# Odd exponentials of a graph attention kernel in two half tiles, added by two GpSimd instructions

## The chip, the cores and the metric

The kernel runs on one core of a Trainium2 chip. The metric is the device time of one execution in microseconds (us), the median of several runs. The engines are named as in the profile: PE is TensorE, DVE VectorE, ACT ScalarE, POOL GpSimd and SP SyncE, which issues DMAs.

## The reference

16 graphs of 1024 nodes with 256 features each, and a 0/1 adjacency matrix for each. Two layers follow each other, layer 0 with 4 heads of 64 features and layer 1 with 8 heads of 32. Each is a masked attention on the normalized input, added to the input:

```python
def gnn(h, adj, Wq, Wk, Wv, Wo, bo):          # per head; D = 64 or 32
    q, k, v = h @ Wq, h @ Wk, h @ Wv          # layer 1: each with a bias
    s = where(adj == 1, q @ k.T / sqrt(D), -inf)
    return concat(softmax(s) @ v) @ Wo + bo

h = relu(layernorm(x));  x = x + gnn(h, adj, *layer0)
h = relu(layernorm(x));  x = x + gnn(h, adj, *layer1)
```

All is in float32.

## The kernel before

**Steps.** For each graph and layer the queries are cut into two halves of 512 and the heads into two groups (class `Group`). Scores are kept transposed, keys on the partitions and queries along the row, so that their exponentials are at once the operand of the product with the values. A step (class `Step`) has four blocks of 128 keys x 512 queries. In layer 0 a group has two heads and a step takes two key tiles; in layer 1 a group has four heads and a step takes one key tile. A group has 4 steps in layer 0 and 8 in layer 1; `st.j` counts them. Of the 768 steps 256 are of layer 0 and 512 of layer 1.

**What a step does.** `scores` (L400) writes the four blocks into two PSUM pairs of two banks each; the pool `ps_s` has three such pairs, which the projections (`pq`, `pv`, `py`) and transposes (`ph`) share. `exponentials` takes one pair after the other: L416 on DVE takes the minimum of the scores and the mask times 1e20 and writes half of the step's tile `p` in SBUF, and L421 on ACT takes the exponential in place. Two steps later (`LEAD = 2`) `weigh` (L433) multiplies the four blocks with the values into one PSUM bank `po`.

**Row sums.** The softmax's denominators are sums of the exponentials over the keys. In layer 1, `count_steps` adds the tile of each odd step onto that of the even step before it with one GpSimd instruction (L534, 128 x 2048 float32). DMAs that add (`accumulate`, L520) then gather the four sums of a group into one tile, and `count` (L301) multiplies it with a matrix of ones. In layer 0, `add_tiles` (L442 to L448) folds two steps into half a tile with DVE and GpSimd instructions.

**Buffers.** An even step's tile comes from seven buffers with the tag `p0`, as it lives until the row sums are done. An odd step's tile comes from two buffers with the tag `p1`, and is free when `weigh` and the add have read it. Before the first steps the same buffers hold the first adjacency matrix (`stage`, `stage_t`).

**Order.** Every engine's instructions stand in the order in which the program issues them; nothing reorders them. `Stream.run` issues the steps of all graphs in one stream, layer 0 of graph b + 1 in front of layer 1 of graph b, and at each step what `later` has put down for it: normalization (L173 to L190), projections, the load of adjacency rows (L128, issued by GpSimd), their transposition by DMA (L134, issued by SP), the conversion to a mask (L143 on ACT, L151 on DVE), the bias (L198, a DMA that GpSimd issues) and the division by the row sums (L341 to L352). GpSimd so has in one queue its adds, the issue of its DMAs and some small instructions, and where the first of them waits, the rest waits too.

Of the kernel before, what the change touches and what calls it, by code (L numbers as in the profile page):

```python
# [10 lines left out]
F32 = mybir.dt.float32  # L11
BF16 = mybir.dt.bfloat16
# [6 lines left out]
P = 128  # L19
# [3 lines left out]
LEAD = 2  # L23
# [59 lines left out]
def fast_program(ctx, tc, a, w, loads, chk):  # L83
# [3 lines left out]
    nc = tc.nc  # L87
    x, adj, out = a["x"], a["adj"], a["out"]
    B, N, E = x.shape
    NT = N // P  # L90
# [6 lines left out]
    pp = ctx.enter_context(tc.tile_pool(name="pp", bufs=2))  # L97
# [21 lines left out]
    class Mask:  # L119
# [10 lines left out]
        def flip(self, t, to=None):  # L130
            if to is None:
                to = adjp.tile([P, NT, P], BF16, tag="adjT", name=f"adjT_{self.b}_{t}")
            self.flipped[t] = to
            nc.sync.dma_start_transpose(to, self.src.pop(t))  # L134
# [137 lines left out]
    class Group:  # L272
# [20 lines left out]
                st.gr, st.j, st.n, st.last = self, j, f"{self.n}_{j}", j == n_j - 1  # L293
                yield st

        def count(self, p, start, stop):

            if start:
                self.s = ps_o.tile([P, 512], F32, tag="pz", name=f"pz_{self.n}")
            for r in range(self.per):  # L300
                nc.tensor.matmul(  # L301
                    self.s[r * self.D : (r + 1) * self.D, :], w.ones[:, : self.D], p[:, r, :],
                    start=start, stop=stop,
                )

        def count_added(self):
            self.count(self.t, True, True)

        def copy_out(self):
            if self.g == 0:  # L310
# [96 lines left out]
    def exponentials(st, between):  # L407


        gr = st.gr  # L410
        odd = st.j % 2
        st.p = pp.tile([P, 4, 512], F32, tag=f"p{odd}", bufs=2 if odd else 7, name=f"p_{st.n}")
        for i in range(2):
            half = st.p[:, ts(i, 2), :]
            kt = st.blocks[2 * i][1]
            nc.vector.scalar_tensor_tensor(  # L416
                out=half,
                in0=gr.mask.m[gr.qh][:, kt, :].unsqueeze(1).to_broadcast([P, 2, 512]),
                scalar=BIG, in1=st.ps[i], op0=ALU.mult, op1=ALU.min,
            )  # L420
            nc.scalar.activation(half, half, AF.Exp, scale=gr.scale)  # L421
            if i == 0:
                for f in between:
                    f()

    def weigh(st):
        gr = st.gr
        D = gr.D
        if st.j == 0:
            gr.o = ps_o.tile([P, 512], F32, tag="po", name=f"po_{gr.n}")  # L430
        for i, (r, kt) in enumerate(st.blocks):
            h = gr.g * gr.per + r
            nc.tensor.matmul(  # L433
                gr.o[r * D : (r + 1) * D, :], gr.inp.v[:, kt, h * D : (h + 1) * D],
                st.p[:, i, :], start=(kt == 0), stop=(kt == NT - 1),
            )

    def add_tiles(one, two):


        a, b = one.p[:, 0:2, :], one.p[:, 2:4, :]
        nc.vector.tensor_add(a, a, b)  # L442

        engine = nc.vector if one.j else nc.gpsimd
        engine.tensor_add(b, two.p[:, 0:2, :], two.p[:, 2:4, :])  # L445
        nc.gpsimd.tensor_add(a, a, b)  # L446
        if one.j:
            nc.gpsimd.tensor_add(a, a, one.gr.t)  # L448
        one.gr.t = a
# [9 lines left out]
    class Stream:  # L459
# [19 lines left out]
        def run(self):  # L479
# [3 lines left out]
            for i in range(n + LEAD):  # L483
# [6 lines left out]
                if i % 2 or not self.large(i):  # L490
                    for st in waiting:
                        weigh(st)
                    for st in waiting:
                        if st.gr.layer:
                            self.count_steps(i, st)
                        if st.last:
                            copies.append(st.gr.copy_out)
                            self.end_group(i, st.gr)
                    waiting = []
# [5 lines left out]
                if now:  # L505
                    exponentials(now, copies)
                else:
                    for f in copies:
                        f()
                if i % 2 and 3 <= i <= n and steps[i - 2].gr.layer == 0:  # L510
                    add_tiles(steps[i - 3], steps[i - 2])
# [10 lines left out]
        def count_steps(self, i, st):  # L522


            gr, j = st.gr, st.j
            if gr.hurry and j >= NT - 2:
                if st.last:
                    self.counted(i, gr)
                gr.count(st.p, False, st.last)
            elif j % 2:  # L530
                one = self.steps[i - LEAD - 1].p
                if not (gr.brief or gr.pairs) and j == 7:
                    self.accumulate(gr.two, gr.one)
                nc.gpsimd.tensor_add(one, one, st.p)  # L534
                if gr.pairs:
                    self.later(i + 2, gr.count, one, j == 1, st.last)
                elif j == 1:
                    gr.one = one
                elif j == 3:
                    self.accumulate(one, gr.one)  # L540
                    gr.one = one
                    if gr.brief:
                        self.later(i + 8, gr.count, one, True, False)
                elif gr.brief:
                    self.later(i + (6 if j == 5 else 4), gr.count, one, False, st.last)
                elif j == 5:
                    gr.two = one
                else:
                    self.later(i + (2 if gr.last else 3), self.accumulate, one, gr.two)
                    self.later(i + (4 if gr.last else 8), gr.count, one, True, True)  # L550

        def counted(self, i, gr):

# [34 lines left out]
    masks = [Mask(b) for b in range(B)]  # L588
# [3 lines left out]


    stage = [pp.tile([P, 4, N], BF16, tag="p0", bufs=7, name=f"adj_0{i}") for i in range(2)]
    stage_t = pp.tile([P, 4, NT, P], BF16, tag="p1", bufs=2, name="adjT_0")

    def load(u):
        masks[0].load(u, stage[u // 4][:, u % 4, :])
# [11 lines left out]

    def flip(u):
        to = stage[0][:, u % 4, :].rearrange("p (t q) -> p t q", q=P)
        masks[0].flip(u, stage_t[:, u, :, :] if u < 4 else to)

    flip(0)
    flip(1)
    open_w(1)
    inp.k(0)
# [6 lines left out]
    mask.put(1)  # L625
    inp.values(0)
    flip(2)
    open_x(1, 0)
    flip(3)
# [52 lines left out]
    for t in range(NT):  # L682
        i = 5 + 2 * t
# [207 lines left out]
def kernel(  # L891
# [28 lines left out]
    with ExitStack() as fast, tc.manual_schedule():  # L920
        fast_program(fast, tc, a, w, loads, chk)
# [61 lines left out]
```

## Time and profile before

| | us |
|---|---|
| median of 3 runs | 3335.38 |
| the runs | 3333.37 to 3335.87 |
| span of the profiled execution | 3332.6 |
| PE busy in it | 3245.0 (97%) |
| DVE busy | 2557.2 (77%) |
| POOL busy | 2387.3 (72%) |
| ACT busy | 2178.2 (65%) |
| L534, 255 instructions | 1201.7 |
| L416, 1536 instructions | 1790.7 |

The span goes from the first to the last instruction of one execution. What lies around it isn't given apart for that execution; the median of the runs is 2.8 us above the span. A row of the page's groups has the line, the engine, the operation, what is written from what, the shape and the count; then busy us and the mean ns of one; then the idle time of the engine just before them, and what ended it. The granted TensorE clock of the profiled execution was 0.993 of full speed on average.

### The profile page before, as it was taken

The page shows a single profiled execution, that of the slowest core. Times are in us where ns is not written, and L with a number is a line of the kernel's source. Part 1 is how long each engine was busy: PE and PEld are TensorE (multiplying, and loading weights), DVE is VectorE, ACT ScalarE, POOL GpSimd, SP SyncE. Part 2 cuts the span into 40 slices and gives each one's busy share as a digit, 9 for nine tenths or more (in the row PEclk, how much of TensorE's full clock was granted, in tenths as well). Part 3 has the DMA queues.
Part 4 walks back from the last instruction along what each step waited for, and adds up shares of the span by engine and source line. Part 5 has one row for each costly group of instructions (what it writes and reads, how often), then busy time and mean ns, then how long its engine had stood idle before and what let it go on. Part 6 is the DMA issues. An engine that isn't in the chain of part 4 may idle for free.

```text
span 3332.6 us, 44087 instructions
## 1 busy us (share of the span) xinstructions
PE 3245.0 (97%) x16766; PEld 1272.4 (38%) x16766; DVE 2557.2 (77%) x2760; ACT 2178.2 (65%) x2402; POOL 2387.3 (72%) x1272
## 2 busy tenths in 40 slices
PE   8999999999999999999999999999999999999898
PEld 3443343433433333333434333343343343333333
DVE  5777877878778787786878768787787877878867
ACT  5567576675766757567575666757667576675565
POOL 4568586786867868677686776868778586785766
PEclk9999999999999999999999999999999999999999
DMA  7338467383664846548375573855738467482431
GB/s 145 63 67 148 97 111 140 73 153 86 121 128 82 157 83 131 113 93 149 77 141 102 105 138 77 146 103 112 138 74 152 96 112 139 80 149 52 89 77 31
DMA packets 313484, 361.08 MB, mean 108 GB/s; under 512 B 190000, under 2 KB 257840, under 8 KB 290480
## 3 DMA queue, kind: packets, MB, share of 16 engines
q0 software_dynamic: 77856, 253.78, 42.1%
q1 hardware_dynamic: 235408, 104.41, 14.0%
q8 instruction: 133, 2.18, 0.3%
q14 instruction: 87, 0.71, 0.1%
HBM read 119.54 MB, written 17.56 MB: 41 GB/s over the span
## 4 chain that ended last, share of the span: by engine, by line
PE 73%; POOL 8%; DMA 7%; DVE 5%; issue 3%; ACT 3%; SPq 1%; POOLq 0%; DVEq 0%; ACTq 0%
PE ps L400 24%; PE po L433 21%; PE pq L225 11%; PE pv L262 7%; PE py L381 5%; POOL p L534 5%; DMA p<-p 4%; DVE p L416 4%; PE pz L301 3%; DMA adjT<-adj 2%; ACT p L421 1%; PE ph L208 1%; POOL p L445 1%; ACT mask L143 1%; DVE p L442 1%
## 5 line engine op out<-in xcount | busy, mean ns | idle before, releaser
L416 DVE SCALAR_TENSOR_TENSOR p<-mask,ps 128x1024 f32<-128x1024 fp8e4 x1536 | 1790.7, 1213 | 598.6 <-PE ps L400 509.9
L421 ACT ACTIVATE p<-p 128x1024 f32<-128x1024 f32 x1536 | 1616.8, 1057 | 960.6 <-DVE p L416 915.2
L534 POOL TENSOR_TENSOR p<-p,p 128x2048 f32<-128x2048 f32 x255 | 1201.7, 4714 | 181.5 <-PE po L433 162.2
L400 PE MATMUL ps<-qT,kT 32*128 32x512 f32 (+1 forms) x6144 | 1196.0, 635 | 37.4 <-DVE p L416 35.6
L433 PE MATMUL po<-p,v 128*32 128x512 f32 (+1 forms) x6144 | 994.0, 603 | 1.0 <-ACT cat L312 0.9
L400 PEld LDWEIGHTS ps<-qT,kT 32*128 32x128 f32 (+1 forms) x6144 | 382.4, 185 | 739.5 <-issue 358.6
L446 POOL TENSOR_TENSOR p<-p 128x1024 f32<-128x1024 f32 x128 | 319.7, 2497 | 273.4 <-DVE p L445 268.4
L433 PEld LDWEIGHTS po<-p,v 128*32 128x32 f32 (+1 forms) x6144 | 229.1, 118 | 691.7 <-issue 503.6
L445 POOL TENSOR_TENSOR p<-p 128x1024 f32<-128x1024 f32 x64 | 151.4, 2366 | 236.2 <-DVE p L442 151.8
L262 PE MATMUL pv<-wv,hT 128*128 128x256 f32 x1024 | 239.5, 387 | 14.6 <-ACT hT L209 14.5
L520 POOL DMA_DIRECT2D p<-p x178 | 178.8, 1005 | 98.1 <-DMA p<-p 66.1
L225 PE MATMUL pq<-hT,wk 128*128 128x512 f32 x512 | 239.6, 611 | 2.8 <-ACT hT L209 2.8
L225 PE MATMUL pq<-hT,wq 128*128 128x512 f32 x512 | 240.0, 612 | 0.1
L381 PE MATMUL py<-wo,cat 128*128 128x256 f32 x1008 | 235.8, 387 | 3.3 <-ACT hT L209 1.0
L262 PEld LDWEIGHTS pv<-wv,hT 128*128 128x128 f32 x1024 | 190.6, 191 | 88.1 <-ACT hT L209 26.8
L381 PEld LDWEIGHTS py<-wo,cat 128*128 128x128 f32 x1008 | 188.3, 191 | 74.7 <-issue 46.3
L352 POOL TENSOR_TENSOR cat<-cat,inv 128x512 f32<-128x512 f32 x127 | 178.8, 1408 | 7.5 <-DMA inv<-vd 6.3
L151 DVE TENSOR_SCALAR mask<-mask 128x1024 fp8e4<-128x1024 fp8e4 x128 | 178.6, 1395 | 0.0
L442 DVE TENSOR_TENSOR p<-p 128x1024 f32<-128x1024 f32 x128 | 161.4, 1261 | 0.0
L448 POOL TENSOR_TENSOR p<-p,p 128x1024 f32<-128x1024 f32 x64 | 152.4, 2381 | 5.0
L301 PE MATMUL pz<-p,ones 128*32 128x512 f32 (+1 forms) x888 | 148.7, 595 | 4.6 <-DMA p<-p 3.8
L225 PEld LDWEIGHTS pq<-hT,wk 128*128 128x128 f32 x512 | 93.2, 192 | 145.1 <-issue 103.5
(50 smaller groups left out, 1696.0 us busy)
## 6 DMA issues: line engine op xcount, KB each, us to landing
p<-p POOLq DMA_DIRECT2D x178, 1024.0 KB, 8.8
adj<-in_adj_dram POOLq DMA_DIRECT2D x128, 256.0 KB, 4.4
x<-bo POOLq DMA_DIRECT2D x64, 512.0 KB, 6.0
x<-in_x_dram SPq DMA_DIRECT2D x32, 512.0 KB, 4.1
inv<-vd SPq DMA_DIRECT2D x128, 128.0 KB, 2.9
inv<-vd SPq DMA_DIRECT2D x252, 64.0 KB, 2.9
out_dram<-x SPq DMA_DIRECT2D x31, 512.0 KB, 3.1
sums<-s SPq DMA_DIRECT2D x384, 2.0 KB, 3.4
```

Source lines behind the costliest of these rows:

```text
L225: nc.tensor.matmul(pq[:, m, :], wt[self.layer][:, c, ts(m, P)], self.hT[half][:, c, :], start=(c == 0), stop=(c == 1),)
L262: nc.tensor.matmul(pv[:, i, :], self.hT[half][:, c, ts(i, P)], w.v[self.layer][:, c, :], start=(c == 0), stop=(c == 1),)
L301: nc.tensor.matmul(self.s[r * self.D : (r + 1) * self.D, :], w.ones[:, : self.D], p[:, r, :], start=start, stop=stop,)
L381: nc.tensor.matmul(py[:, i, :], self.half.cat[:, c, ts(i, P)], w.o[self.layer][:, c, :], start=(c == 0), stop=(c == 1),)
L400: nc.tensor.matmul(st.ps[i // 2][:, i % 2, :], gr.inp.kT[r * D : (r + 1) * D, gr.g, ts(kt, P)], gr.inp.qT[gr.qh][r * D : (r + 1) * D, gr.g ...
L416: nc.vector.scalar_tensor_tensor(out=half, in0=gr.mask.m[gr.qh][:, kt, :].unsqueeze(1).to_broadcast([P, 2, 512]), scalar=BIG, in1=st.ps[i] ...
L421: nc.scalar.activation(half, half, AF.Exp, scale=gr.scale)
L433: nc.tensor.matmul(gr.o[r * D : (r + 1) * D, :], gr.inp.v[:, kt, h * D : (h + 1) * D], st.p[:, i, :], start=(kt == 0), stop=(kt == NT - 1),)
L442: nc.vector.tensor_add(a, a, b)
L445: engine.tensor_add(b, two.p[:, 0:2, :], two.p[:, 2:4, :])
L446: nc.gpsimd.tensor_add(a, a, b)
L534: nc.gpsimd.tensor_add(one, one, st.p)
```

## The change

In an odd step the exponentials are written into two tiles of 128 x 2 x 512 instead of one of 128 x 4 x 512, with the tags `p10` and `p11` and two buffers each, so that the memory is the same. `count_steps` adds each of them onto its half of the even step's tile with an instruction of its own. An even step keeps its one tile, and `st.halves` names its two halves. `weigh`, `count`, `add_tiles` and the first adjacency's `stage_t` read the halves in place of the whole. In the built program every other instruction keeps its place on its engine; each half add waits for TensorE and ScalarE as the whole one did, and the first and the second half of L416 in an odd step each wait for GpSimd's add of the buffer that they write.

```diff
-        def count(self, p, start, stop):
+        def count(self, halves, start, stop):
...
-                    self.s[r * self.D : (r + 1) * self.D, :], w.ones[:, : self.D], p[:, r, :],
+                    self.s[r * self.D : (r + 1) * self.D, :], w.ones[:, : self.D],
+                    halves[r // 2][:, r % 2, :],
...
-            self.count(self.t, True, True)
+            self.count([self.t], True, True)
...
-        st.p = pp.tile([P, 4, 512], F32, tag=f"p{odd}", bufs=2 if odd else 7, name=f"p_{st.n}")
-        for i in range(2):
-            half = st.p[:, ts(i, 2), :]
+        if odd:
+            st.halves = [
+                pp.tile([P, 2, 512], F32, tag=f"p1{i}", bufs=2, name=f"p_{st.n}_{i}")
+                for i in range(2)
+            ]
+        else:
+            st.p = pp.tile([P, 4, 512], F32, tag="p0", bufs=7, name=f"p_{st.n}")
+            st.halves = [st.p[:, ts(i, 2), :] for i in range(2)]
+        for i, half in enumerate(st.halves):
...
-                st.p[:, i, :], start=(kt == 0), stop=(kt == NT - 1),
+                st.halves[i // 2][:, i % 2, :], start=(kt == 0), stop=(kt == NT - 1),
...
-        engine.tensor_add(b, two.p[:, 0:2, :], two.p[:, 2:4, :])
+        engine.tensor_add(b, *two.halves)
...
-                gr.count(st.p, False, st.last)
+                gr.count(st.halves, False, st.last)
             elif j % 2:
-                one = self.steps[i - LEAD - 1].p
+                even = self.steps[i - LEAD - 1]
+                one = even.p
                 if not (gr.brief or gr.pairs) and j == 7:
                     self.accumulate(gr.two, gr.one)
-                nc.gpsimd.tensor_add(one, one, st.p)
+                for k, half in enumerate(st.halves):
+                    nc.gpsimd.tensor_add(one[:, ts(k, 2), :], one[:, ts(k, 2), :], half)
...
-    stage_t = pp.tile([P, 4, NT, P], BF16, tag="p1", bufs=2, name="adjT_0")
+    stage_t = [
+        pp.tile([P, 2, NT, P], BF16, tag=f"p1{i}", bufs=2, name=f"adjT_0{i}") for i in range(2)
+    ]
...
-        masks[0].flip(u, stage_t[:, u, :, :] if u < 4 else to)
+        masks[0].flip(u, stage_t[u // 2][:, u % 2, :, :] if u < 4 else to)
```

The other calls of `count` pass `even.halves` where they passed `one`.

More of the change, by code (lines that the diff above doesn't have):

```diff
@@ L528, in count_steps @@
                     self.counted(i, gr)
-                gr.count(st.p, False, st.last)
+                gr.count(st.halves, False, st.last)
             elif j % 2:
-                one = self.steps[i - LEAD - 1].p
+                even = self.steps[i - LEAD - 1]
+                one = even.p
                 if not (gr.brief or gr.pairs) and j == 7:
                     self.accumulate(gr.two, gr.one)
-                nc.gpsimd.tensor_add(one, one, st.p)
+                for k, half in enumerate(st.halves):
+                    nc.gpsimd.tensor_add(one[:, ts(k, 2), :], one[:, ts(k, 2), :], half)
                 if gr.pairs:
-                    self.later(i + 2, gr.count, one, j == 1, st.last)
+                    self.later(i + 2, gr.count, even.halves, j == 1, st.last)
                 elif j == 1:
@@ L542, in count_steps @@
                     if gr.brief:
-                        self.later(i + 8, gr.count, one, True, False)
+                        self.later(i + 8, gr.count, even.halves, True, False)
                 elif gr.brief:
-                    self.later(i + (6 if j == 5 else 4), gr.count, one, False, st.last)
+                    self.later(i + (6 if j == 5 else 4), gr.count, even.halves, False, st.last)
                 elif j == 5:
@@ L549, in count_steps @@
                     self.later(i + (2 if gr.last else 3), self.accumulate, one, gr.two)
-                    self.later(i + (4 if gr.last else 8), gr.count, one, True, True)
+                    self.later(i + (4 if gr.last else 8), gr.count, even.halves, True, True)
         def counted(self, i, gr):
```

## The prediction

> **What bounds the kernel now.** I read the page first: the totals, then the groups of layer 1, then the list of waits, then one stretch in order of time.
>
> ```profile
> span 3332.6 us, 44087 instructions
> ...
> PE 3245.0 (97%) x16766; PEld 1272.4 (38%) x16766; DVE 2557.2 (77%) x2760; ACT 2178.2 (65%) x2402; POOL 2387.3 (72%) x1272
> ...
> L416 DVE SCALAR_TENSOR_TENSOR p<-mask,ps 128x1024 f32<-128x1024 fp8e4 x1536 | 1790.7, 1213 | 598.6 <-PE ps L400 509.9
> ...
> L534 POOL TENSOR_TENSOR p<-p,p 128x2048 f32<-128x2048 f32 x255 | 1201.7, 4714 | 181.5 <-PE po L433 162.2
> ...
> L448 POOL TENSOR_TENSOR p<-p,p 128x1024 f32<-128x1024 f32 x64 | 152.4, 2381 | 5.0
> ```
>
> TensorE sets the end: 97% busy, nobody else over 77%. A gain has to be TensorE time. The page's last three rows give the parts: the masking on VectorE (L416), the whole-tile add that the change splits (L534), and an add of half that size (L448). The waits of VectorE show where L534 reaches the others:
>
> ```profile
> DVE p L416 <- PE ps L400: 509.9, 343, 5.0
> ...
> DVE p L416 <- POOL p L534: 83.1, 61, 3.2
> ```
>
> The columns are total us, times, longest. In 61 of the 255 cases VectorE stands before an odd step because the odd buffer, of which there are two, has not been read by GpSimd yet. What that costs TensorE is in the timeline of one such stretch (start, length, engine, line, idle time before):
>
> ```profile
> 2144.83 4.57 POOL L534 TENSOR_TENSOR p<-p,p 128x2048 f32<-128x2048 f32 x1
> ...
> 2149.43 4.61 DVE L416 SCALAR_TENSOR_TENSOR p<-mask,ps 128x1024 f32<-128x1024 fp8e4 x4 [1.54 <-POOL p L534]
> ...
> 2153.41 0.66 POOL L128 DMA_DIRECT2D adj<-in_adj_dram  x1 [4.01 <-DMA adjT<-adj]
> ...
> 2154.65 4.91 POOL L534 TENSOR_TENSOR p<-p,p 128x2048 f32<-128x2048 f32 x1
> ...
> 2155.47 1.14 PE L400 MATMUL ps<-qT,kT 32*128 32x512 f32 x8
> ...
> 2158.40 1.13 PE L400 MATMUL ps<-qT,kT 32*128 32x512 f32 x4
> ...
> 2159.15 1.63 POOL L352 TENSOR_TENSOR cat<-cat,inv 128x512 f32<-128x512 f32 x1
> 2159.59 4.61 DVE L416 SCALAR_TENSOR_TENSOR p<-mask,ps 128x1024 f32<-128x1024 fp8e4 x4 [2.79 <-POOL p L534]
> ...
> 2160.37 4.90 POOL L534 TENSOR_TENSOR p<-p,p 128x2048 f32<-128x2048 f32 x1
> ...
> 2160.87 1.13 PE L400 MATMUL ps<-qT,kT 32*128 32x512 f32 x4 [1.34 <-DVE p L416]
> ```
>
> The scores of a step are eight matmuls into two PSUM pairs. At 2155.47 both pairs were free and the eight ran side by side; the next work began 1.07 us later. At 2158.40 only one was: its four ran, then TensorE stood until VectorE had emptied the other, the second four began at 2160.87 and the next work at 2161.92. That is 3.52 us for 1.07, a loss of 2.45, though the idle column says 1.34. Added over the 512 score stretches of layer 1, the time above 1.07 is 147 us, and 72 us of it lie in the 60 stretches where VectorE's lateness goes back to a wait for L534. They come in 15 groups, one in each batch but the last, 3.4 to 6.8 us each. So 72 us is the ceiling.
>
> **What the Trainium skill says.** "Perfetto Trace Analysis", Identifying Performance Opportunities: an equal gap that comes back again and again can mean too few buffers. The trace agrees: two odd buffers, 61 waits. The same page, Optimizing Scalar/DVE Operations, says that if an engine isn't saturated but causes bubbles on others, cutting its instructions up may let work finish sooner; that is the change's pattern, said there of other engines. "GPSIMD Engine Reference", Performance versus the Vector engine, has 4497 ns for an add of 2048 float32 columns; here the shortest L534 took 4525 ns. "Advanced Engine Details and Errata", VectorE Performance Modes, says GpSimd and VectorE's two-port instructions block each other. The trace has that at L151: 661 ns at the shortest, 8427 at the longest, the latter ending 0.6 us after an L534 had.
>
> **The change, part by part.**
>
> *The adds.* 255 adds of 2048 columns become 510 of 1024. Shortest whole add 4525 ns; shortest 1024-column add on GpSimd 2342 (L446, L445 2341, L448 2344). Two halves are 4.68, so **0.16 us more per pair**. Back to back nothing of that hides: the L534 at 2160.37 follows L352, which ended at 2160.78, and ended 4.49 after it. 255 x 0.16 = 41 us more GpSimd work, 72% to 73% busy. Outside the 15 groups it costs nothing: GpSimd then waits for TensorE (162.2 us over 111 times at L534). If that cover failed everywhere it would be the 41 us.
>
> *The release.* Call E the end of the whole add. Before, VectorE's first half starts at E and its second at E + 1.13 (four L416 in 4.61). After, the first half may start at E + 0.16 - 2.34, the second at E + 0.16. Where VectorE's wait is under 2.2 us, the first half waits no more. But the second half can't pass E, and all that follows it on VectorE's queue (the next even step, which frees the PSUM pairs of the next scores and projections) is behind it. So relative to GpSimd, VectorE wins **at most 1.13 us, and once**: the next odd step meets the next E, and E moves only if GpSimd starts earlier.
>
> *Does E move?* In the group shown it doesn't. The add at 2154.65 is queued behind L128, which waited 4.01 us for a transposing DMA that was issued at 2148.85, before the first wait of the group ended. The add at 2160.37 follows it through L352 without a break. In the group at 1939 to 1961 the add at 1950.68 is behind an accumulating DMA (L520), issued 0.6 us after the one issued at 1939.71 landed (1949.5), itself behind an add. Both are GpSimd's own chain.
>
> *Worked through for 2144 to 2168.* First wait, 1.54: E = 2149.40, first half free from 2147.2, VectorE ready at 2147.9: gone, TensorE 1.04 ahead. Second: E = 2159.56 becomes 2159.72; VectorE is ready at 2155.8, its first half starts at 2157.4, its second at 2159.72, and the following masks end 1.13 - 0.16 = 0.97 sooner than before. Third: two splits in the chain, E = 2165.27 becomes 2165.59; the values' matmuls, which take the PSUM pair of the second half, start at 2165.59 + 1.25 = 2166.84 instead of 2167.71, some 0.8 sooner. Then GpSimd catches up. Gain of the group: 1.13 - 2 x 0.16 = **0.81 us**, of 5.2 lost. Times 15: 12.2 us. I take 0.81 for all. With three splits in the chain a group gives 0.65 (10 us), with one 0.97 (14.5 us).
>
> *The rest.* The second half of L416 gets a wait of its own for GpSimd: a semaphore event of 21 ns (median), at most 384 odd steps x 21 ns = 8 us on an engine with 23% idle, taken as nothing; on the chain in the groups it is 15 x 2 x 0.02 = 0.6 us. The half-tile reads at L433 and L301 and the three-operand forms at L445 are the same instructions. SBUF is the same size, as is the order on every queue. DMAs keep number and size; L520 is issued up to 0.16 later. In the last batch two L151 stand 8.4 and 6.3 us behind GpSimd's queue; each has one split add in its way: 0.3 us more if VectorE doesn't get in between the halves, 2 x 2.3 us less if it does. I take 0.
>
> Sum: span 3332.6 - 12.2 + 0.6 = 3321.0. The median of the runs shown is 2.8 above this profile's span (3335.38), so 3323.8; I say 3323.
>
> **The rivals.**
> *Every wait shrinks by itself.* If E follows TensorE in most groups (GpSimd's gaps ahead of L128 and L520 move along), each of the 61 waits gives up the smaller of itself and 1.13 us: 51 of the 83 us of waiting. At the rate of the ceiling (72 lost for 83 waited) that is 44 us: 3291. For it: in each group GpSimd does have gaps of 2 to 4 us. Against: their releasers are DMAs.
> *Nothing to measure.* The second half is what TensorE needs next, or the pair costs 0.4 rather than 0.16, so a group gives 0 to 0.4: 3330 to 3336.
> *Slower, by the shared port.* L151 loses against GpSimd's queue when two adds follow without a gap; now there are twice as many starts, and all have shifted. One more L151 held for two instructions costs 6 to 8 us, as at 3115 and 3156. The gain of 12 is gone with two such, and it is a measurable loss from three on, out of the six L151 of the last batch that take 0.7 to 1.8 us now: 3323 + 3 x 7 = 3344. For it: those two are the longest stalls of TensorE in the trace (7.2 and 5.3 us). Against: in the other batches L151 meets the adds of layer 0, which keep their size.
> *The change doesn't do what it says*: only if the second half had to wait for the first's add; the built program has the two tiles waiting each for its own. Left at nothing.
>
> **How the numbers follow.** A measurement of this kernel tells about 0.2%, 6.7 us, from no change. One allowance a group (gain 7 to 25): 0.58. Every wait (25 to 60): 0.14. Nothing: 0.21. Shared port: 0.07. So faster 0.72, same 0.21, slower 0.07. The range 3296 to 3334 leaves out the upper end of the second case, the losses, and the last part of the third.
>
> **What would show it.** Right: L534's successor has 510 instructions near 2.36 us, some 41 us more GpSimd time; the wait of L416 for it falls well below 83 us but stays, now before second halves; the sum over score stretches drops by about 12. Wrong: that wait nearly gone and TensorE's stretches at 1.07 (second case); pairs over 4.9 us (third); a longer L151 (fourth).

## The result and the profile after

The kernel after took 3348.3 us (median of 20 runs, 3343.4 to 3360.3), the kernel before in the same comparison 3340.6 us (20 runs, 3333.4 to 3356.3). The ratio is **1.0022, with a 95% interval of 1.0010 to 1.0034**: slower by about 7.7 us. The forecast was 3323 us, with a range of 3296 to 3334. It stood on 3335.4 us for the kernel before, the median of the three runs shown above, so it was a gain of 12 us.

The profile's page of the kernel after (totals, then groups: line, engine, operation, what is written from what, shape, count | busy us, mean ns | idle us before them and what ended most of it):

```profile
span 3349.0 us, 44964 instructions
...
PE 3236.8 (97%) x16766; PEld 1272.0 (38%) x16766; DVE 2582.6 (77%) x2760; ACT 2180.3 (65%) x2402; POOL 2425.2 (72%) x1527
...
L423 DVE SCALAR_TENSOR_TENSOR p<-mask,ps 128x1024 f32<-128x1024 fp8e4 x1536 | 1794.6, 1213 | 593.7 <-PE ps L401 519.0
...
L543 POOL TENSOR_TENSOR p<-p,p 128x1024 f32<-128x1024 f32 x510 | 1245.4, 2562 | 145.9 <-PE po L440 145.9
...
L262 PE MATMUL pv<-wv,hT 128*128 128x256 f32 x1024 | 239.1, 387 | 30.2 <-DVE p L423 15.5
...
L225 PE MATMUL pq<-hT,wq 128*128 128x512 f32 x512 | 239.9, 612 | 9.6 <-DVE p L423 9.5
...
L151 DVE TENSOR_SCALAR mask<-mask 128x1024 fp8e4<-128x1024 fp8e4 x128 | 202.6, 1583 | 0.0
...
L301 PE MATMUL pz<-p,ones 128*32 128x512 f32 (+1 forms) x888 | 150.0, 602 | 21.5 <-DMA p<-p 20.6
```

The line numbers that moved: L352 is now L353, L400 is L401, L416 is L423, L442 to L446 are L449 to L453, L520 is L527 and L534 is L543. TensorE has the same matmuls and is busy 8 us less, yet the span is 16 us longer. GpSimd has 38 us more work. The last two rows are the ones to look at, since the change touches neither. Before they were:

```profile
L151 DVE TENSOR_SCALAR mask<-mask 128x1024 fp8e4<-128x1024 fp8e4 x128 | 178.6, 1395 | 0.0
...
L301 PE MATMUL pz<-p,ones 128*32 128x512 f32 (+1 forms) x888 | 148.7, 595 | 4.6 <-DMA p<-p 3.8
```

L151, a conversion of the mask on VectorE, takes 24 us more, and L301, the product with ones that gives the row sums, stands 17 us longer for the accumulating DMA.

The waits of the kernel after (total us, times, longest):

```profile
DVE p L423 <- POOL p L543: 69.8, 63, 3.3
...
PE pz L301 <- DMA p<-p: 20.6, 14, 3.7
...
PE pv L262 <- DVE p L423: 15.5, 13, 1.2
...
PE pq L225 <- DVE p L423: 9.5, 13, 1.2
```

Instruction by instruction on VectorE, the 83 us before first halves have become 25 us before first halves and 45 us before second ones. The second halves' wait comes out at `pv` and `pq`, the projections that take the PSUM pair of the second half: 1.2 us each at most. And L301 waits in 14 batches, 0.26 to 3.65 us each; before, the same 14 waits were 0.22 to 0.64 us.

Since the 16,766 matmuls stand in the same order in both traces, the intervals from one start to the next can be subtracted one by one, and the differences summed by what the later matmul writes. Before to after that gives scores -25.1 us, `pv` +15.3, `pq` +9.5, `pz` (L301) +17.4, the rest -0.9: together +16.2, nearly all of the 16.4 us between the two spans. **What the scores won, the projections gave back, and the row sums lost 17 us on top.**

### How a late GpSimd reaches the row sums

One of the 14, in order of time (start, length, engine, line, idle time before). Before:

```profile
548.41 4.53 POOL L534 TENSOR_TENSOR p<-p,p 128x2048 f32<-128x2048 f32 x1 [0.61 <-PE po L433]
...
552.90 0.59 POOL L128 DMA_DIRECT2D adj<-in_adj_dram  x1
...
553.32 2.04 DVE L151 TENSOR_SCALAR mask<-mask 128x1024 fp8e4<-128x1024 fp8e4 x1
553.50 1.30 POOL L352 TENSOR_TENSOR cat<-cat,inv 128x512 f32<-128x512 f32 x1
...
559.11 1.22 DVE L442 TENSOR_TENSOR p<-p 128x1024 f32<-128x1024 f32 x1
...
565.23 0.87 POOL L520 DMA_DIRECT2D p<-p  x1
...
572.29 1.06 PE L301 MATMUL pz<-p,ones 128*32 128x512 f32 x8 [0.23 <-DMA p<-p]
```

After:

```profile
552.13 4.96 POOL L543 TENSOR_TENSOR p<-p,p 128x1024 f32<-128x1024 f32 x2
...
555.65 3.81 DVE L151 TENSOR_SCALAR mask<-mask 128x1024 fp8e4<-128x1024 fp8e4 x1
556.76 0.85 POOL L128 DMA_DIRECT2D adj<-in_adj_dram  x1
557.36 1.54 POOL L353 TENSOR_TENSOR cat<-cat,inv 128x512 f32<-128x512 f32 x1
...
562.97 1.21 DVE L449 TENSOR_TENSOR p<-p 128x1024 f32<-128x1024 f32 x1
...
569.54 0.85 POOL L527 DMA_DIRECT2D p<-p  x1
...
577.29 1.93 PE L301 MATMUL pz<-p,ones 128*32 128x512 f32 x8 [2.89 <-DMA p<-p]
```

VectorE comes to L151 with the scores, 2.33 us later than before, as TensorE does at this point. GpSimd comes out of this multiplication (L352, L353) 4.1 us later (558.90 against 554.80), so it is 1.8 us late against TensorE: it is still in the last add of layer 1 when L151 comes. In both traces L151 ends 0.56 us after it, however long before it began. So GpSimd's 1.8 us go into L151 (2.04 to 3.81 us). Of these, 1.5 us reach the fold of layer 0 on VectorE (L442, later L449) and GpSimd's fold behind it. There GpSimd's second instruction takes 0.4 us more, and the DMA that adds takes 7.7 us from its issue to its landing in place of 7.0. TensorE, which before had waited 0.23 us at this place, now waits 2.89.

The same is found in 13 of the 14 batches (in the last one nothing changes). Their second L151 takes 0.4 to 2.2 us more, the fold behind it comes later by that less 0.1 to 0.3 us, and in nine of them L301 comes later by what the fold is late, within 0.03 us. In the other four GpSimd's fold or the DMA adds 0.5 to 1.5 us. TensorE's own time from L151 to the matmul ahead of L301 is the same in both traces. The 0.23 us is the point: the chain **already ended at TensorE in each of the 14 batches before the change**, and of what is added to it nearly all is lost.

### The profile page after: what moved, and what is told of

Its sections match the earlier page's. It is cut to its first block, busy times and chain, and to the rows that moved or that the text cites. A ratio compares the mean times of both kernels' runs of the same rounds, so it can differ in the third digit from the quotient of the medians.

```text
span 3349.0 us, 44964 instructions
## 1 busy us (share of the span) xinstructions
PE 3236.8 (97%) x16766; PEld 1272.0 (38%) x16766; DVE 2582.6 (77%) x2760; ACT 2180.3 (65%) x2402; POOL 2425.2 (72%) x1527
## 3 DMA queue, kind: packets, MB, share of 16 engines
q8 instruction: 133, 2.18, 0.3%
## 4 chain that ended last, share of the span: by engine, by line
PE 73%; POOL 7%; DMA 7%; DVE 6%; issue 4%; ACT 3%; SPq 1%; POOLq 0%; DVEq 0%; ACTq 0%
PE ps L401 24%; PE po L440 21%; PE pq L225 11%; PE pv L262 7%; PE py L382 5%; POOL p L543 4%; DVE p L423 4%; DMA p<-p 4%; PE pz L301 3%; DMA adjT<-adj 2%; ACT p L428 1%; PE ph L208 1%; POOL p L452 1%; DVE mask L151 1%; ACT mask L143 1%
## 5 line engine op out<-in xcount | busy, mean ns | idle before, releaser
L423 DVE SCALAR_TENSOR_TENSOR p<-mask,ps 128x1024 f32<-128x1024 fp8e4 x1536 | 1794.6, 1213 | 593.7 <-PE ps L401 519.0
L543 POOL TENSOR_TENSOR p<-p,p 128x1024 f32<-128x1024 f32 x510 | 1245.4, 2562 | 145.9 <-PE po L440 145.9
L401 PE MATMUL ps<-qT,kT 32*128 32x512 f32 (+1 forms) x6144 | 1186.4, 635 | 21.0 <-DVE p L423 19.2
L401 PEld LDWEIGHTS ps<-qT,kT 32*128 32x128 f32 (+1 forms) x6144 | 380.8, 184 | 715.0 <-issue 332.9
L453 POOL TENSOR_TENSOR p<-p 128x1024 f32<-128x1024 f32 x128 | 321.0, 2507 | 259.8 <-DVE p L452 254.8
L452 POOL TENSOR_TENSOR p<-p,p 128x1024 f32<-128x1024 f32 x64 | 151.6, 2368 | 253.5 <-ACT p L428 95.2
L262 PE MATMUL pv<-wv,hT 128*128 128x256 f32 x1024 | 239.1, 387 | 30.2 <-DVE p L423 15.5
L527 POOL DMA_DIRECT2D p<-p x178 | 178.1, 1001 | 107.3 <-DMA p<-p 58.0
L151 DVE TENSOR_SCALAR mask<-mask 128x1024 fp8e4<-128x1024 fp8e4 x128 | 202.6, 1583 | 0.0
L353 POOL TENSOR_TENSOR cat<-cat,inv 128x512 f32<-128x512 f32 x127 | 182.8, 1439 | 9.0 <-DMA inv<-vd 8.3
L301 PE MATMUL pz<-p,ones 128*32 128x512 f32 (+1 forms) x888 | 150.0, 602 | 21.5 <-DMA p<-p 20.6
L449 DVE TENSOR_TENSOR p<-p 128x1024 f32<-128x1024 f32 x128 | 161.9, 1265 | 0.0
L455 POOL TENSOR_TENSOR p<-p,p 128x1024 f32<-128x1024 f32 x64 | 151.8, 2372 | 5.0
L225 PEld LDWEIGHTS pq<-hT,wq 128*128 128x128 f32 x512 | 93.4, 192 | 153.7 <-issue 118.6
```

Of the source, the lines that this page charges most:

```text
L151: nc.vector.tensor_scalar(m, m, -0.5, 0.5, op0=ALU.not_equal, op1=ALU.subtract, saturate=False)
L225: nc.tensor.matmul(pq[:, m, :], wt[self.layer][:, c, ts(m, P)], self.hT[half][:, c, :], start=(c == 0), stop=(c == 1),)
L262: nc.tensor.matmul(pv[:, i, :], self.hT[half][:, c, ts(i, P)], w.v[self.layer][:, c, :], start=(c == 0), stop=(c == 1),)
L301: nc.tensor.matmul(self.s[r * self.D : (r + 1) * self.D, :], w.ones[:, : self.D], halves[r // 2][:, r % 2, :], start=start, stop=stop,)
L401: nc.tensor.matmul(st.ps[i // 2][:, i % 2, :], gr.inp.kT[r * D : (r + 1) * D, gr.g, ts(kt, P)], gr.inp.qT[gr.qh][r * D : (r + 1) * D, gr.g ...
L423: nc.vector.scalar_tensor_tensor(out=half, in0=gr.mask.m[gr.qh][:, kt, :].unsqueeze(1).to_broadcast([P, 2, 512]), scalar=BIG, in1=st.ps[i] ...
```

## The experiments

Theory A: the loss is GpSimd's lateness, carried through the second conversion (L151) of each batch to the row sums. Rivals: the price of cutting the add alone makes the loss; the two long stalls of the last batch hide the gain; the odd buffers are too few. All kernels were compared with the kernel before on the same chip.

**1. The cut without the release.** The kernel before, with one odd tile, its add in two instructions:

```diff
-                nc.gpsimd.tensor_add(one, one, st.p)
+                for k in range(2):
+                    nc.gpsimd.tensor_add(one[:, ts(k, 2), :], one[:, ts(k, 2), :], st.p[:, ts(k, 2), :])
```

> The kernel before, with its one tile for an odd step, but the add of 2048 columns cut into two adds of 1024. So the cost of the cut alone, without the earlier release. Theory A (GpSimd's queue, late by 0.16 us for each cut add, reaches TensorE at the row sums of the last group through the mask instruction L151 of VectorE): ratio to before 1.002 to 1.006, as the changed kernel or a little more; TensorE's idle time before the row sums (L301) 10 us or more against 4.6. Rival C (the cost of the changed kernel lies in the second halves' own wait, ahead of the projections): ratio 1.000 to 1.001, as there is no such wait here.

Measured: 3337.3 us, ratio 0.9976 (0.9963 to 0.9989), span 3324.5. Up to 3114 us into the execution it was 7.3 us behind the kernel before; then it gained 15.5 us, 12.8 of them because the two L151 of the last batch came in a pause of GpSimd (2.2 us at L352, for a DMA) and while it issued a DMA, and took 1.5 and 0.7 us where they had taken 8.4 and 6.3. The whole ratio so says little about the cut: these two stalls hang on a few microseconds of timing. Later kernels take them out.

Theory A expected 10 us or more of idle time ahead of L301, and that failed: it is 6.9 us, against 4.6 before and 21.5 with the half tiles. The place that was shown above, in this kernel:

```profile
550.83 4.68 POOL L535 TENSOR_TENSOR p<-p,p 128x1024 f32<-128x1024 f32 x2 [0.62 <-PE po L433]
...
555.77 2.14 DVE L151 TENSOR_SCALAR mask<-mask 128x1024 fp8e4<-128x1024 fp8e4 x1
...
556.07 1.28 POOL L352 TENSOR_TENSOR cat<-cat,inv 128x512 f32<-128x512 f32 x1
```

GpSimd has the same cut adds as in the kernel after, but it waits for TensorE ahead of the last of them (0.62 us, before 0.61), and L151 takes 2.14 us. Over the 13 batches the last add of layer 1 starts 4.90 us before L151 in the kernel before, 4.88 to 4.94 with the cut alone, and 3.04 to 4.90 with the half tiles, where GpSimd has no idle time ahead of it. The multiplication of the group before it (L352, L353) starts at the median 29.8, 29.9 and 28.8 us before L151. So **the cut adds do not make GpSimd late at L151; the early release does, as it lets TensorE and VectorE come there 1.0 us sooner than GpSimd can follow**. At L151 this has become 0.4 to 2.2 us, as GpSimd waits in between for the DMAs that add, which land sooner or later. From here on theory A is tested in this narrower form.

**2 and 3. The second conversion moved out of GpSimd's way**, from step 2 of each batch's layer 0 to its step 15, in the kernel after and, as a control, in the kernel before:

```diff
-        for i, u in zip((0, 2, 4, 6, 8, 10, 12, 13), range(NT)):
+        for i, u in zip((0, 15, 4, 6, 8, 10, 12, 13), range(NT)):
             later(a + i, masks[b].second, u)
```

> The changed kernel, but in each batch the second of the eight mask instructions L151 (tiles 2 and 3 of the first half of the queries) is issued at step 15 of the layer-0 stretch instead of step 2. Theory A: L151 no longer stands behind GpSimd's last add and L353 at that place, VectorE isn't held, the 17 us more of waits before the row sums go: idle before L301 under 8 us, time 12 to 17 us under the changed kernel's, ratio to before 0.997 to 0.999. Rival B (the accumulating DMAs, each behind the landing of the one before, are late by themselves): idle before L301 stays over 15 us, ratio 1.001 to 1.004. Rival C: the same as B.

> The control: the kernel before with the same one mask instruction moved from step 2 to step 15. Theory A: the waits before the row sums are 4.6 us here, so at most that much is to be had: ratio 0.998 to 1.000. Rivals B and C: 1.000, within 0.1%.

Measured: the half tiles 3327.1 us, 0.9944 (0.9925 to 0.9964); the whole tile 3345.8 us, 1.0007 (0.9989 to 1.0025). The row of L301 in the half-tile kernel:

```profile
L301 PE MATMUL pz<-p,ones 128*32 128x512 f32 (+1 forms) x888 | 148.7, 596 | 4.7 <-DMA p<-p 3.9
```

21.5 us of idle time have become 4.7. The same move is worth nothing to the whole tile, where 4.6 us became 6.3. The half tiles gain 26 us on the kernel after by the ratios, where 12 to 17 were expected. L301 has 17 of them; the mean granted clock, 0.9946 against 0.9924 in the kernel after, goes with some 7 more (an estimate, from the 3.3 us for each 0.001 below).

**4. A price in GpSimd alone.** The kernel after with each half add cut again, to 512 columns:

```diff
-                    nc.gpsimd.tensor_add(one[:, ts(k, 2), :], one[:, ts(k, 2), :], half)
+                    for h in range(2):
+                        q = one[:, 2 * k + h, :]
+                        nc.gpsimd.tensor_add(q, q, half[:, h, :])
```

> The changed kernel with each half add cut again, four adds of 512 columns for an odd step: some 0.3 us more GpSimd time per pair of steps, the same tiles and releases. Theory A: what GpSimd is late by grows from about 1.1 us at that place in a batch to about 3, and all of it arrives at the row sums: 20 to 35 us over the changed kernel, ratio 1.008 to 1.013. Rival C: the later ends hold the second halves alone, 15 groups x 2 x 0.3 = 9 us over the changed kernel, ratio 1.005. If GpSimd's lateness doesn't matter: 1.002.

Measured: 3370.5 us, 1.0077 (1.0049 to 1.0105). GpSimd is busy 73 us more than in the kernel after, and the ratio is 0.0055 higher, 18 us: `pz` stands 27.6 us (21.5), `pq` 18.8 (9.6), `pv` 31.8 (30.2). Theory A expected 20 to 35 us, all of it at the row sums. The sum came close, but only 6 us of it stand there and 9 at `pq`, ahead of the projections. More GpSimd work that releases no buffer earlier is lost in part, and mostly at these two places.

**5, 6 and 7. All conversions moved**, those of experiment 2 and, in the last batch, the two that had stalled 8.4 and 6.3 us:

```diff
-            for u in range(NT):
-                later(c + 8 + 2 * u, masks[b + 1].second, u)
+            for i, u in zip((8, 12, 12, 14, 16, 20, 20, 22), range(NT)):
+                later(c + i, masks[b + 1].second, u)
```

with the whole tile, the half tiles, and the whole tile with the cut add of experiment 1:

> The kernel before with three mask instructions L151 taken out of GpSimd's way: the second of each batch at step 15 of the layer-0 stretch, and in the last batch the second at step 12 instead of 10 and the sixth at step 20 instead of 18 after the start of layer 1. The last two are the ones that stood 8.4 and 6.3 us. Theory A: 12 us less than before, ratio 0.995 to 0.998; both then take under 2 us. If those two stalls are hidden: 1.000.

> The changed kernel with the same three moves. Theory A: 12 us under the version that has only the first move (0.9944): ratio 0.990 to 0.993, so 4 to 8 thousandths under the kernel before with the same moves. That difference is the worth of the two half tiles once VectorE isn't held: the prediction on record said 12 us, 0.36%. If the half tiles are worth nothing: equal to the kernel before with the same moves.

> One tile for an odd step, the add cut into two, and the same three moves. The bare price of the cut, with the lucky or unlucky stalls of L151 out of the way. Theory A: 15 stretches by two or three cuts of 0.16 us, 5 to 8 us over the kernel before with the same moves (ratio to before 0.997 to 1.000). If cutting the add is a gain by itself, as the first run of it (0.9976) can be read: at or under the kernel before with the same moves. If that run's gain was the two stalls of the last batch alone, which it missed: over it.

Measured: whole tile **3322.9** us, 0.9944 (0.9921 to 0.9967); half tiles **3309.0** us, 0.9904 (0.9881 to 0.9926); whole tile with two adds 3329.1 us, 0.9961 (0.9950 to 0.9973). So by the medians the cut by itself costs 6 us, the early release brings 20, and together they are worth 14 us once no conversion stands in GpSimd's way. The intervals of the whole tile's two ratios overlap, so the 6 us are not clear of the noise; the traces, below, give 8.4. The half tiles with the moved conversions are faster than both kernels. Their waits and rows:

```profile
DVE p L423 <- POOL p L543: 66.1, 64, 2.0
...
PE pz L301 <- DMA p<-p: 4.7, 14, 1.3
```

```profile
L262 PE MATMUL pv<-wv,hT 128*128 128x256 f32 x1024 | 237.8, 385 | 32.4 <-DVE p L423 16.7
...
L225 PE MATMUL pq<-hT,wq 128*128 128x512 f32 x512 | 236.7, 605 | 10.0 <-DVE p L423 9.8
```

The second halves' waits and what they cost `pv` and `pq` are as in the kernel after. Only `pz` differs.

**8. More odd buffers.** The kernel after with three buffers for each odd half and, for the memory, six even ones in place of seven (the first adjacency's tiles, which share them, have the same numbers):

```diff
-                pp.tile([P, 2, 512], F32, tag=f"p1{i}", bufs=2, name=f"p_{st.n}_{i}")
+                pp.tile([P, 2, 512], F32, tag=f"p1{i}", bufs=3, name=f"p_{st.n}_{i}")
...
-            st.p = pp.tile([P, 4, 512], F32, tag="p0", bufs=7, name=f"p_{st.n}")
+            st.p = pp.tile([P, 4, 512], F32, tag="p0", bufs=6, name=f"p_{st.n}")
```

> The changed kernel with three buffers for each odd half tile and six instead of seven for the even tiles (the memory is full). Theory A: VectorE's waits for the half adds (70 us) and the waits before the projections (25 us more than before) go, but GpSimd's queue is as late as ever at the row sums and VectorE is still held at L151, so what is won in the scores comes back before L301: ratio 0.997 to 1.003, idle before L301 over 20 us. If the waits for the buffers are what costs: ratio 0.985 to 0.992. If six even tiles are too few: new waits of L423 for the DMAs that add, and over 1.003.

Measured: 3390.9 us, 1.0136 (1.0111 to 1.0162). The new wait is at the even tiles:

```profile
DVE p L423 <- DMA p<-p: 129.4, 37, 11.8
```

VectorE's wait for the half adds fell from 70 to 4.5 us, and the waits of `pv` and `pq` for it went, as expected. But memory that is taken from the even tiles costs far more than the wait for GpSimd. The idle time ahead of L301 is 6.4 us here, where theory A expected over 20; in a kernel that is slowed down elsewhere TensorE may have no lead to give back, which no run here shows. Whether a third odd buffer alone would help stays open: with seven even tiles there is no memory for it.

**9 and 10. Only the last batch's conversions moved**, the second edit of experiments 5 to 7 without the first. This asks which of the two moves turned the sign:

> The whole tile with only the two conversions of the last batch moved (L151 at 3115 and 3156); the second conversion of every other batch stays where GpSimd's queue holds it. Both theories: about 12 us less than the kernel before, from the two stalls of TensorE of 7.2 and 5.3 us, so a ratio near 0.996, and the idle time ahead of L301 stays near 5 us.

> The half tiles with the same two conversions moved. Theory A (GpSimd's 1.1 us of lateness reaches TensorE through the second conversion of the other 14 batches and the row sums behind it): the half tiles stay slower than the whole tile here, by 5 to 10 us (ratio near 0.998 to 0.999 against the kernel before), with 20 us of idle time ahead of L301, where with all conversions moved they were 14 us faster. Theory B (the last batch's conversions are what hid the gain): the half tiles are 10 to 14 us faster than the whole tile here too, ratio near 0.992.

Measured: whole tile 3324.2 us, 0.9948 (0.9931 to 0.9965); half tiles 3326.4 us, 0.9952 (0.9935 to 0.9969). The half tiles, first:

```profile
L151 DVE TENSOR_SCALAR mask<-mask 128x1024 fp8e4<-128x1024 fp8e4 x128 | 192.0, 1502 | 0.0
...
L301 PE MATMUL pz<-p,ones 128*32 128x512 f32 (+1 forms) x888 | 150.4, 604 | 20.5 <-DMA p<-p 19.6
```

and the whole tile:

```profile
L151 DVE TENSOR_SCALAR mask<-mask 128x1024 fp8e4<-128x1024 fp8e4 x128 | 166.8, 1304 | 0.0
...
L301 PE MATMUL pz<-p,ones 128*32 128x512 f32 (+1 forms) x888 | 148.7, 595 | 6.3 <-DMA p<-p 5.4
```

The theory of the last batch falls: the half tiles are not 10 to 14 us faster here, and the two medians can't be told apart. Theory A has the idle time ahead of L301 right (20 us expected, 20.5 measured), but its ratio of 0.998 to 0.999 was missed: 2 us of loss instead of 5 to 10. Moving one conversion per batch besides takes the difference between half tiles and whole tile from +2 to -14 us. That is 16 us, the size of the loss at L301. Why +2 and not more may be the clock, which follows.

### What the granted clock adds

The profile gives a granted TensorE clock with each run. Over 39 runs of the kernel before on one chip it lay between 0.987 and 0.994, and the time fell by 3.3 us for each 0.001 of clock, which is that share of the time in full. The kernels' means differ as well:

| whole tile, then half tiles | mean us | mean clock | difference us | at equal clock (estimate) |
|---|---|---|---|---|
| second conversion moved (3, 2) | 3345.6, 3327.7 | 0.9906, 0.9946 | -17.9 | -4.7 |
| all conversions moved (5, 6) | 3324.4, 3310.0 | 0.9944, 0.9972 | -14.4 | -5.2 |
| last batch's moved (9, 10) | 3325.3, 3327.2 | 0.9935, 0.9968 | +1.9 | +12.8 |

The last column adds 3.3 us for each 0.001 by which the half tiles' clock was higher. By this estimate the second conversion's place is again worth 17 to 18 us, the half tiles' own gain is 5 us, and the rest of the 14 is clock. For the last pair it may be too high: the comparison of intervals in the next section gives +1.3 us for it at full clock, though it leaves out 5.4 us of L301's stalls, which touch stretches at half clock.

"TensorE: Matmul & The Clock Gate", Part 1, in the Trainium skill explains such a clock: it is halved after an idle window of about 3.4 us and restored after a busy one, and the windows run freely. The traces here agree on the length, but a window need not be idle for it. The stall at L301 shown above, in windows of the time (length, busy us of each engine with counts, granted clock, DMA share, GB/s):

```profile
573.20:576.60 3.40, 1.20 (x6) 0.14 (x2) 1.58 (x2) 1.54 (x2) 1.59 (x1) 1.00 0.98 212
576.60:583.40 6.80, 6.11 (x18) 1.68 (x20) 1.63 (x2) 1.45 (x2) 3.64 (x3) 0.50 0.69 181
```

TensorE was busy for 1.20 of 3.40 us, and the next 6.8 us ran at half clock. In six traces (before and after, and kernels 5, 6, 9 and 10), all 32 stretches at half clock that begin before 3295 us last one, two or three times 3.41 us and begin after a window in which TensorE had been busy at most 0.78 of the time. Not every such window is followed by one. So one stall can be paid for twice, by this reading. The longest stalls of before were the two in the last batch, and without them (kernel 9) the clock after them is whole, before first:

```profile
3122.50:3132.70 10.20, 8.11 (x20) 4.96 (x21) 6.12 (x6) 5.13 (x5) 1.19 (x2) 0.50 0.51 103
3163.50:3170.30 6.80, 6.50 (x16) 3.75 (x17) 4.33 (x5) 5.13 (x5) 0.00 (x0) 0.50 0.76 153
```

```profile
3122.50:3132.70 10.20, 9.25 (x54) 4.73 (x53) 10.10 (x12) 5.01 (x6) 8.07 (x3) 1.00 0.83 150
3163.50:3170.30 6.80, 6.75 (x31) 2.06 (x26) 6.30 (x6) 5.46 (x6) 6.50 (x3) 1.00 0.61 129
```

That the half tiles' shorter waits leave fewer windows idle enough (nine units of 3.41 us at half clock in kernel 5, one in kernel 6) fits this. No run changed the clock alone, so it is argued, not shown.

## Why the prediction was wrong

To take the clock out of the sum as well, the intervals between matmuls were compared again, leaving out those in which either run stood at half clock:

| us | scores | `pv` and `pq` | `pz` | sum |
|---|---|---|---|---|
| before to after | -28.4 | +24.1 | +14.4 | +9.6 |
| the same with all conversions moved (5 to 6) | -30.7 | +25.1 | +0.2 | -6.5 |
| the cut alone (5 to 7) | +7.2 | +0.5 | +1.2 | +8.4 |
| the release alone (7 to 6) | -37.1 | +25.8 | -1.0 | -13.1 |

Sums include small terms that have no column. Each row compares two single executions.

- **The adds.** Forecast 510 instructions near 2.36 us and 41 us more. Right: the median is 2.38, the row grew from 1201.7 to 1245.4 us.
- **"Then GpSimd catches up."** This is the step that failed. The prediction let TensorE and VectorE win up to 1.13 us on GpSimd in each group, and took it that they keep them. GpSimd had less slack than that in most batches: ahead of its last add of layer 1 it had waited for 0.0 to 1.4 us before the change, 0.69 at the median. With the half tiles this idle time is gone, the add is still running or has just ended when the second L151 comes, and L151 stands behind GpSimd's queue. The prediction looked for waits of L416 for GpSimd and for nothing else that stands behind it. What TensorE had won it gave back at L301: 14.4 us at full clock, 17.4 in all, against the 13.1 that the release brings.
- **"Outside the 15 groups it costs nothing"**, said of the cut's 41 us, held at this place for the cut alone: `pz` lost 1.2 us from 5 to 7 and 2.3 us in experiment 1.
- **The rival by the shared port** had the right instruction in the wrong place. It put L151's loss into the last batch and said against itself that in the others L151 meets only adds of layer 0. The trace of before denies that: at 553.32, as in 12 other batches, the second L151 takes 2.03 to 2.18 us against 0.66 for the shortest, with the issue of a DMA and L352 above it and a layer 1 add just ended. In the last batch, where the rival looked, the two L151 took 8.7 and 6.3 us after and 8.4 and 6.3 before: as taken, 0.
- **At most 1.13 us, and once.** Right in kind: first halves' waits fell from 83 to 25 us, second halves' rose to 45, and the projections behind them wait up to 1.2 us. In size, the release brought 13.1 us at full clock, 0.87 a group; and the cut cost 8.4, 0.56 a group where 2 x 0.16 = 0.32 was taken. What is left in the groups (scores with `pv` and `pq`) is 4.3 to 5.6 us, **0.3 to 0.4 a group where 0.81 stood**. Which groups had three or four cuts in their chain was not taken apart.
- **Every wait shrinks by itself (3291).** Fell: 70 us of the 83 stayed.
- **The doubt that the second half is what TensorE needs next** ("Nothing to measure", a group gives 0 to 0.4) was the best description of the groups. Alone it would have given 3330 to 3336.
- **The sum.** 12.2 forecast for the groups was 4.3 at full clock, and 14.4 to 17.4 at L301 was not in the sum. The signs that the prediction named did not warn of it: the time of score stretches above 1.07 us fell from 147 to 137, near the 12 foretold, while `pv`, `pq` and `pz`, which that measure leaves out, lost 42.

On the lock itself, "Advanced Engine Details and Errata", VectorE Performance Modes, says that the two engines block each other and not for how long. "SBUF — State Buffer", SBUF: two separate sides, says that whoever starts first has the pair for the whole instruction. In these runs the loser was at times held for more than one: L151 at 555.65 lasted through the rest of a half add, a DMA issue and a multiplication. That the lock is what holds it is argued from the times; no run takes the lock away alone.

## What to carry to other kernels

When a change lets the bound engine get ahead of an engine with slack, the lead is kept only where that engine catches up before its work is needed. So look in the trace of before for how long it waits for the bound engine there (here 0.0 to 1.4 us), and for every place where a chain through it ends at the bound engine with almost no gap (here 0.23 us), also far from the code that is changed. An early release of half a buffer is worth at most what the second half's consumer leaves of it, once for each group. If it is still wanted, first move what stands behind the late engine: here, with three conversions moved in both kernels, the half tiles' loss of 8 us became a gain of 14 on the whole tile, of which 5 to 6.5 us are left when the clock is taken out.

## What the hardware showed unexpectedly

- An L151 that meets GpSimd's work takes 0.66 us at the shortest and 8.7 us at the longest. In the kernels before and after, each of the 170 that took over 0.72 us ended 0.55 to 0.56 us after the end of a GpSimd add or multiplication, but not always of the first: 2 of 83 before and 16 of 87 after were held through more than one. Nor does it take a pause of GpSimd: at 391.03 of the kernel before, L151 ended while the next multiplication (L352) stood in the trace as running, and that one took 1.73 us in place of the 1.30 at 553.50. Cutting an add into two back-to-back instructions did not let VectorE in between them in the last batch of the kernel after (8.7 us against 8.4 before); in experiment 1 it got in where GpSimd waited 2.2 us for a DMA.
- A GpSimd add takes at the shortest 1.25 us for 512 columns, 2.34 for 1024 and 4.53 for 2048. From the last two, each instruction has about 0.16 us that does not shrink with its size, also back to back: two of 1024 columns took 4.68 us together at 550.83 in experiment 1.
- A window of 3.41 us in which TensorE is busy for 0.6 to 0.7 of the time can be enough to halve its clock for the next one, at most a further 1.7 us by half of that length (an estimate). Most such windows in the six traces have no half clock behind them.
